# The end of a four-layer kernel: which engine does a 20-tap convolution and the gates' second product, and in which order

## The chip, the cores and the metric

The kernel runs on one core of a Trainium2 chip. A core has five engines, each with its own in-order queue of instructions: TensorE (PE in the profile; PEld is its weight load), VectorE (DVE), ScalarE (ACT), GpSimd (POOL) and SyncE (SP), which here issues transfers alone. TensorE writes to PSUM, which is split into eight banks of 128 partitions x 512 f32; the rest lies in SBUF. The metric is the device time of one execution in microseconds (us). Everything is f32.

## The reference, cut to what matters

The program is four layers of attention and feed-forward over 4096 tokens of 128 channels (8 blocks of 512 tokens). The change touches the last layer (layer 3) alone, which reads, for each block of tokens `x`:

```python
xn = layernorm(x)                     # attention: a causal depthwise convolution
h  = sum(table[:, i] * shift(xn, i) for i in range(1, 21))   # tap 0 is zero
x  = x + xn @ W1 + h @ W2 + bias
q  = fp4(layernorm(x))                # feed-forward, all operands rounded to fp4
g  = silu(q @ fp4(w_gate).T) * (q @ fp4(w_up).T)      # 352 wide
x  = x + fp4(g) @ fp4(w_down).T
```

`fp4` takes blocks of 16 numbers, scales each by its largest magnitude over 6, rounds to the eight fp4 magnitudes and scales back.

## The kernel before, in words

Layers 0 and 1 come first. Then `late()` (L1351) runs layer 2's attention as 64 frames (8 blocks x 8 pairs of heads), and hangs the other work on them: `at(frame, hook, f)` (L1369) puts a step into a frame, and the loop at L1984 calls the steps of its frame at four fixed places. Layer 3 of block b follows its attention by some frames; `planned` (L1822) gives every step of a block its frame. All instructions are issued in the order in which the code calls them (`manual_schedule`); each engine takes its own in that order, and an instruction that waits holds back all behind it on its engine.

When the 64 frames are over, `end()` (L1891) runs what is left in an order that is written out by hand. Left are: the last context and output product of attention; the feed-forward of block 6, called `L` below, from its gates on; and all of layer 3 for block 7, the last, in two halves: `A` (token tiles 0 and 1) and `B` (tiles 2 and 3). A tile is 128 tokens. The steps, each a function of `layer3` (L1647) or `norm_steps` (L1377):

- `stats` / `stats2` (L1382): VectorE's batch statistics, then on GpSimd the reciprocal root (L243, L244) and the shift (L1393). `scale` / `scale2` (L1395): ScalarE normalises, one activation per tile (L1399); the first one also adds the bias to `x` on GpSimd (L1407). `turn_` (L1414): TensorE transposes the tiles (L1417), ScalarE copies them into `xp`, the padded, channel-major input of the convolution (L1418).
- The convolution of a half, 20 taps. Taps 1 to 12 on TensorE: `conv_p` (L1685) multiplies shifted windows of `xp` with `tap_w[i]`, which is `W2` with each row scaled by tap i; these twelve matrices are made on ScalarE in frames 25 to 36 (`tap_weights` L1622, L1886 to L1889). Taps 13 to 16 on VectorE (`conv_v` L1662), taps 17 to 20 as ScalarE products (L1682) that GpSimd sums (L1683, `conv_s` L1673). `join` (L1698) adds the two sums, `conv_out` (L1709) multiplies the sum with `W2` into the same PSUM bank and adds the bank to `x` on VectorE (L1702). Blocks 0 to 6 have all taps on VectorE, ScalarE and GpSimd.
- `quant_x1` / `quant_x2` (L1722, L1726): fp4 of the normalised half. `fp4_scale` (L1255) is four VectorE instructions (L1265, L1267, L1268, L1270) and one of GpSimd (L1269); `fp4_round` (L1273) is four of VectorE (L1281, L1284, L1285, L1286) and a product on GpSimd (L1287). `turn_x` (L1730): transpose (L1733) and ScalarE copy (L1735).
- `gated(j)` (L1744): two 128x352 matmuls, then `tanh` on ScalarE into `s` (L1755; `s` has two buffers). `gated_v(j)` is `rest()` (L1757): two VectorE instructions, `(s+1)*gate` (L1758) and `s*0.5*up` into `h` (L1759).
- `quant_h1(i)`, `quant_h2(i)`: fp4 of a pair of `h` tiles, 704 wide; the scale and the scaled copy of this width have one buffer, so the next `quant_h1` waits until GpSimd has finished the product of the last `quant_h2`. `turn_h(i)` (L1784): three transposes per tile (L1790) and two ScalarE copies (L1793, L1796). `down` (L1798): twelve matmuls (24 in the profile, which counts an f32 matmul of this width twice) for a block, six for a half, the add to `x` on VectorE and the store.

PSUM in `late()` (L2016): two double banks `two` (the scores', `bank2()`), one bank `c`, one `o`, and two single banks `one` (`bank()`), used in turn. In `end()`, A's convolution takes `c` and B's takes `o`; the gates of A and B take double banks, and those of L take the single ones, which `turn_`, `turn_x`, `turn_h` and `down` use as well.

Of the kernel before, what the change touches and what calls it, by code (L numbers as in the profile page):

```python
# [24 lines left out]
P = 128  # L25
# [135 lines left out]
def body(ctx, tc, dram, spans, x_in, ib, it, ic, ei, out):  # L161
# [84 lines left out]
    def mm(out_, lhs, rhs, start=True, stop=True):  # L246
        nc.tensor.matmul(out_, lhs, rhs, start=start, stop=stop)  # L247
# [17 lines left out]
    def cols(t, j):  # L265
        return t[:, j * P : (j + 1) * P]
# [1084 lines left out]
    def late():  # L1351
# [11 lines left out]
        with tc.tile_pool(name="a2", bufs=2) as wp, tc.tile_pool(name="l3", bufs=1) as lp:  # L1363
# [255 lines left out]
            turned_taps = tuple(range(1, 13))  # L1619
            tap_w = {}  # L1620

            def tap_weights():  # L1622
                w = lp.tile([P, 4, TB], F32, tag="cg", name="tapw")
                for k, i in enumerate(turned_taps):
                    tap_w[i] = w[:, k // 4, (k % 4) * P : (k % 4 + 1) * P]
                    yield lambda i=i: nc.scalar.activation(
                        tap_w[i], l3["w2"], AF.Copy, scale=l3["taps"][:, i : i + 1]
                    )
# [18 lines left out]
            def layer3(b, xp, tile_, part=(0, J), conv_bank="one", h_tag="h"):  # L1647
# [37 lines left out]
                def conv_p(*taps):  # L1685

                    t["conv"] = ps = bank(conv_bank)
                    for j in range(j0, j1):
                        for i in (0, *taps):
                            mm(  # L1690
                                cols(ps, j),
                                xp()[:, pad - i + j * P : pad - i + (j + 1) * P],
                                tap_w[i] if i else l3["w1"],
                                start=(j == j0 and i == 0),
                                stop=False,
                            )
# [47 lines left out]
                def gated(j):  # L1744

                    h = tile_("h", h_tile)
                    if whole:
                        pg, pu = bank(), bank()
                    else:
                        two = bank2()  # L1750
                        pg, pu = two[:, 0, :], two[:, 1, :]
# [3 lines left out]
                    nc.scalar.activation(s, pg[:, :I3], AF.Tanh, scale=0.5)  # L1755

                    def rest():  # L1757
                        nc.vector.scalar_tensor_tensor(s, s, 1.0, pg[:, :I3], ALU.add, ALU.mult)  # L1758
                        nc.vector.scalar_tensor_tensor(  # L1759
                            h[:, j, :], s, 0.5, pu[:, :I3], ALU.mult, ALU.mult  # L1760
                        )
# [129 lines left out]
            def end():  # L1891
# [14 lines left out]
                L.gated(0)  # L1906
                A.scale()
                L.gated_v(0)
                A.turn_()
                L.gated(1)  # L1910
                B.scale()
                L.gated_v(1)
                B.turn_()
                L.gated(2)
                A.conv_p(*turned_taps)
                A.conv_v(*range(13, 17))
                A.conv_s(*range(17, 21))
                L.gated_v(2)
                L.gated(3)
                B.conv_p(*turned_taps)  # L1920
                L.quant_h1(0)
                B.conv_v(*range(13, 17))
                B.conv_s(*range(17, 21))
                A.join()
                A.conv_out()
                A.stats2()
                L.gated_v(3)
                L.quant_h2(0)
                B.join()
                A.scale2()  # L1930
                B.conv_out()
                B.stats2()
                A.quant_x1()
                A.quant_x2()
                L.turn_h(0)
                B.scale2()
                L.quant_h1(1)
                A.turn_x()
                A.gated(0)
                A.gated(1)  # L1940
                B.quant_x1()
                B.quant_x2()
                A.gated_v(0)
                A.gated_v(1)
                B.turn_x()
                L.quant_h2(1)
                A.quant_h1(0)
                B.gated(2)
                B.gated(3)
                B.gated_v(2)  # L1950
                A.quant_h2(0)
                L.turn_h(1)
                B.gated_v(3)
                L.down()
# [91 lines left out]
```

## Time and profile before

| | us |
|---|---|
| median of three runs | 1515.44 (1513.49 to 1515.67) |
| the profiled execution, its own time | 1513.91 |
| its span, first to last instruction | 1512.1 |
| the frames end: last output product of attention done | 1445.5 |
| from there to the end of the span | 66.6 |

The times below are from the span's start. In the span TensorE is busy 94%, VectorE 68%, ScalarE 69% and GpSimd 42%. What happens in the last 67 us, by the order of time of the four engines:

| | starts at us |
|---|---|
| A's convolution on TensorE | 1453.18 |
| A's add of the convolution (VectorE L1702) | 1466.62 |
| B's add of the convolution | 1473.46 |
| B's input quantised from | 1480.00 |
| A's `h` quantised from | 1489.68 |
| B's `h` quantised from | 1497.57 |
| last add to `x` | 1508.70 |
| last store issued | 1509.15 |

A row of the order of time reads: start, duration, engine, line, operation, written tile <- read tiles, shape, count, and in brackets how long the engine had been idle and who released it.

### The profile page before, as it was taken

What the parts mean: (1) busy time and instruction counts of PE and PEld (TensorE: products, weight loads), DVE (VectorE), ACT (ScalarE), POOL (GpSimd) and SP (SyncE); (2) the same over time, 40 slices, a digit from 0 to 9 for tenths busy, and PEclk for the clock granted to TensorE, in tenths of its full rate; (3) what the DMA queues carried; (4) which work ended last, traced back from release to release, by engine and by line L of the source; (5) the groups of instructions that cost most, each with busy time, mean ns of one, the idle gap of its engine ahead of it and who ended that gap; (6) DMA issues with size and microseconds to landing.
All of it is one profiled execution on the core that took longest, in us unless ns stands there. A gap on an engine that the chain in (4) does not pass through costs nothing.

```text
span 1512.1 us, 22428 instructions
## 1 busy us (share of the span) xinstructions
PE 1416.4 (94%) x7782; PEld 681.7 (45%) x7782; DVE 1031.1 (68%) x2129; ACT 1047.6 (69%) x2141; POOL 642.4 (42%) x742
## 2 busy tenths in 40 slices
PE   7789999998789889999999999999999999999976
PEld 3652222222276655543444445444454454454454
DVE  6766667777476646661674397786886877868857
ACT  7869999988776545564876486776776767767632
POOL 6647666665564321110441163452442633514432
PEclk9999999999999889999999999999999999999996
DMA  5049999977311010000100000000000000000000
GB/s 182 1 63 129 133 126 129 130 117 106 106 64 29 11 29 1 0 1 0 28 1 1 1 1 7 1 1 8 1 1 8 1 8 1 0 8 1 1 8 14
DMA packets 25442, 55.11 MB, mean 36 GB/s; under 512 B 5265, under 2 KB 18129, under 8 KB 20850
## 3 DMA queue, kind: packets, MB, share of 16 engines
q1 hardware_dynamic: 24688, 51.99, 20.6%
q10 hardware_dynamic: 578, 1.57, 0.3%
q8 instruction: 62, 1.02, 0.3%
q14 instruction: 50, 0.41, 0.1%
q0 software_dynamic: 64, 0.13, 0.0%
HBM read 47.35 MB, written 6.32 MB: 35 GB/s over the span
## 4 chain that ended last, share of the span: by engine, by line
PE 68%; ACT 13%; DVE 11%; DMA 4%; issue 2%; POOL 1%; SPq 0%; DVEq 0%; POOLq 0%; ACTq 0%
PE ps L247 65%; ACT hm L556 5%; DMA gs<-gates 3%; ACT ex L1483 2%; ACT hm L555 2%; DVE pr L568 1%; DVE nm L1477 1%; DVE fm L1284 1%; ACT xn L1399 1%; POOL rs L244 1%; DVE s L702 1%; DMA gates<-eq 1%; DVE frc L1267 1%; ACT xn L713 0%; PE ps L1790 0%
## 5 line engine op out<-in xcount | busy, mean ns | idle before, releaser
L1483 ACT ACTIVATE ex<-ps,nm 128x512 f32<-128x512 f32 x512 | 346.3, 689 | 192.3 <-DVE nm L1477 192.3
L1477 DVE TENSOR_REDUCE nm<-ps 128x2 f32<-128x1024 f32 x256 | 300.6, 1215 | 48.2 <-PE ps L247 47.9
L247 PE MATMUL ps<-q,k 64*128 64x512 f32 x1024 | 258.5, 621 | 4.9 <-ACT ex L1483 4.0
L247 PE MATMUL ps<-ex,vs 128*64 128x512 f32 x1024 | 233.8, 598 | 0.0
L1498 POOL TENSOR_TENSOR vs<-v,sm 128x256 f32<-128x256 f32 x128 | 81.3, 635 | 338.0 <-DVE sm L1497 290.3
L574 POOL TENSOR_TENSOR acc<-acc,pr 128x512 f32<-128x512 f32 x119 | 166.4, 1399 | 108.0 <-DVE pr L568 103.2
L556 ACT ACTIVATE hm<-ps,blob_f 128x1536 f32<-128x1536 f32 x128 | 196.4, 1534 | 0.0
L247 PE MATMUL ps<-xt,blob_a 128*128 128x512 f32 x304 | 151.9, 626 | 0.1
L247 PE MATMUL ps<-h,w 32*128 32x512 f32 x1024 | 148.0, 639 | 3.7 <-DVE eq L467 2.0
L247 PE MATMUL ps<-hm,w 128*32 128x512 f32 x1024 | 136.4, 605 | 11.6 <-DVE pr L568 10.8
L247 PEld LDWEIGHTS ps<-q,k 64*128 64x128 f32 x1024 | 87.5, 186 | 131.2 <-issue 75.3
L568 DVE SCALAR_TENSOR_TENSOR pr<-ps,blob_f,gs 128x512 f32<-128x512 f32 x120 | 89.9, 749 | 74.8 <-PE ps L247 62.3
L1683 POOL TENSOR_TENSOR acs<-acs,prod 128x512 f32<-128x512 f32 (+1 forms) x104 | 129.9, 1249 | 14.3 <-ACT prod L1682 9.6
L247 PEld LDWEIGHTS ps<-ex,vs 128*64 128x64 f32 x1024 | 67.8, 136 | 144.5 <-issue 124.9
L555 ACT ACTIVATE hm<-ps,blob_f 128x512 f32<-128x512 f32 x128 | 88.1, 688 | 29.3 <-PE ps L247 29.1
L243 POOL TENSOR_SCALAR rs<-mv 128x4 f32<-128x4 f32 (+1 forms) x69 | 17.5, 254 | 208.8 <-DVE mv L1389 146.5
L1483 ACT ACTIVATION_READ_ACCUMULATOR ex<-ps,nm 128x1 f32 x512 | 105.6, 206 | 0.0
L1445 DVE TENSOR_TENSOR v<-ps,blob_bc 128x512 f32<-128x512 f32 x64 | 44.3, 692 | 70.7 <-PE ps L247 44.1
L247 PEld LDWEIGHTS ps<-xt,blob_a 128*128 128x128 f32 x304 | 53.0, 193 | 87.5 <-issue 60.2
L247 PEld LDWEIGHTS ps<-h,w 32*128 32x128 f32 x1024 | 40.9, 183 | 111.8 <-ACT hm L555 86.1
L247 PEld LDWEIGHTS ps<-blob_a,ct 128*128 128x128 f32 x512 | 67.0, 191 | 32.3 <-issue 29.2
L244 POOL TENSOR_TENSOR rs<-rs,half 128x4 f32<-128x4 f32 (+1 forms) x69 | 72.4, 1049 | 5.7
(292 smaller groups left out, 2267.6 us busy)
## 6 DMA issues: line engine op xcount, KB each, us to landing
gs<-gates SPq DMA_DIRECT2D x256, 128.0 KB
blob_f<-in_f SPq DMA_DIRECT2D x1, 2560.0 KB
blob_a<-in_a SPq DMA_DIRECT2D x1, 2056.0 KB
x<-in_x SPq DMA_DIRECT2D x8, 256.0 KB
gates<-eq SPq DMA_DIRECT2D x8, 256.0 KB
by_rows<-fxn SPq DMA_DIRECT2D x8, 256.0 KB
ge<-gates SPq DMA_DIRECT2D x4, 512.0 KB
out<-x SPq DMA_DIRECT2D x7, 256.0 KB
```

Source lines behind the costliest of these rows:

```text
L243: nc.gpsimd.tensor_scalar(t, var, EPS, None, ALU.add)
L244: nc.gpsimd.tensor_tensor(t, t, half[:, : t.shape[-1]], ALU.pow)
L247: nc.tensor.matmul(out_, lhs, rhs, start=start, stop=stop)
L555: nc.scalar.activation(hm[:, 0, :], p1, AF.Gelu, bias=bias)
L556: nc.scalar.activation(hm[:, 1:, :], p3, AF.Gelu, bias=bias)
L568: nc.vector.scalar_tensor_tensor(pr, po, f0["b2"][:, e : e + 1], gs, ALU.add, ALU.mult)
L574: nc.gpsimd.tensor_tensor(acc[:, b, :], acc[:, b, :], pr, ALU.add)
L1445: nc.vector.tensor_tensor(v, pv, bias, ALU.add)
L1477: nc.vector.tensor_reduce(nm, ps, AX.X, ALU.max, negate=True)
L1483: nc.scalar.activation(ex[kt][:, i, :], ps[:, i, :], AF.Exp, bias=nm[:, i : i + 1], accum_out=sm[:, kt, i : i + 1],)
L1498: nc.gpsimd.tensor_tensor(vs[:, tiles, :, :], vs_[n][:, tiles, :].rearrange("p j (i n) -> p j i n", i=2), sm[:, tiles, :].unsqueeze(3).to_ ...
L1683: nc.gpsimd.tensor_tensor(t["acs"], t["acs"], p, ALU.add)
```

## The change

Five edits, all in `late()`:

1. `turned_taps` goes from taps 1 to 12 to taps 1 to 20; the eight more matrices are made by ScalarE in frames 37 to 44, four of them in a new tile `tapx` of 128x512.
2. In `end()`, `conv_p`, `conv_v`, `conv_s`, `join` and `conv_out` give way to `conv_tile(j)`, which does `W1` and all 20 taps of one tile on TensorE, and `conv_added()`, the add to `x`. (`conv_p` without taps stays for the other blocks.)
3. `gated(j, True)`, used for L, A and B in `end()`: ScalarE copies half of `up` from PSUM into a `prod` buffer, and GpSimd multiplies it with `s` into `h`, in place of VectorE's second instruction.
4. L's gates in `end()` take the double banks.
5. The order of `end()` is new. Among other things, `L.quant_h1(0)`, `L.quant_h2(0)` and `L.quant_h1(1)` stand ahead of A's add; A's `turn_x` behind B's second convolution tile; `L.turn_h(1)` and `L.down()` ahead of `A.gated_v(0)`; `A.quant_h1(0)`, `A.quant_h2(0)` behind B's gates and ahead of `B.gated_v(2)`.

```diff
@@ -1616,13 +1616,15 @@
 
             pad = 20
 
-            turned_taps = tuple(range(1, 13))
+            turned_taps = tuple(range(1, 21))
             tap_w = {}
 
             def tap_weights():
                 w = lp.tile([P, 4, TB], F32, tag="cg", name="tapw")
+                more = lp.tile([P, TB], F32, tag="tapx", name="tapx")
                 for k, i in enumerate(turned_taps):
-                    tap_w[i] = w[:, k // 4, (k % 4) * P : (k % 4 + 1) * P]
+                    part = w[:, k // 4, :] if k < 16 else more
+                    tap_w[i] = cols(part, k % 4)
                     yield lambda i=i: nc.scalar.activation(
                         tap_w[i], l3["w2"], AF.Copy, scale=l3["taps"][:, i : i + 1]
                     )
@@ -1682,18 +1684,33 @@
                             nc.scalar.activation(p, src, AF.Copy, scale=w)
                             nc.gpsimd.tensor_tensor(t["acs"], t["acs"], p, ALU.add)
 
-                def conv_p(*taps):
+                def conv_p():
 
                     t["conv"] = ps = bank(conv_bank)
                     for j in range(j0, j1):
-                        for i in (0, *taps):
-                            mm(
-                                cols(ps, j),
-                                xp()[:, pad - i + j * P : pad - i + (j + 1) * P],
-                                tap_w[i] if i else l3["w1"],
-                                start=(j == j0 and i == 0),
-                                stop=False,
-                            )
+                        mm(
+                            cols(ps, j),
+                            xp()[:, pad + j * P : pad + (j + 1) * P],
+                            l3["w1"],
+                            start=(j == j0),
+                            stop=False,
+                        )
+
+                def conv_tile(j):
+
+                    if j == j0:
+                        t["conv"] = bank(conv_bank)
+                    for i in (0, *turned_taps):
+                        mm(
+                            cols(t["conv"], j),
+                            xp()[:, pad - i + j * P : pad - i + (j + 1) * P],
+                            tap_w[i] if i else l3["w1"],
+                            start=(j == j0 and i == 0),
+                            stop=(j == j1 - 1 and i == turned_taps[-1]),
+                        )
+
+                def conv_added():
+                    added(t["conv"])
 
                 def join():
                     nc.vector.tensor_tensor(t["acc"], t["acc"], t["acs"], ALU.add)
@@ -1741,10 +1758,10 @@
                     flat = wide.rearrange("p a t -> p (a t)")
                     return flat[:, : J * I3].rearrange("p (j i) -> p j i", j=J)
 
-                def gated(j):
+                def gated(j, at_end=False):
 
                     h = tile_("h", h_tile)
-                    if whole:
+                    if not at_end:
                         pg, pu = bank(), bank()
                     else:
                         two = bank2()
@@ -1753,12 +1770,18 @@
                     mm(pu[:, :I3], cols(t["xt"], j - j0), wt["up"])
                     s = lp.tile([P, I3], F32, tag="s", name="s", bufs=2)
                     nc.scalar.activation(s, pg[:, :I3], AF.Tanh, scale=0.5)
+                    if at_end:
+                        u = block("prod", 3)()[:, :I3]
+                        nc.scalar.activation(u, pu[:, :I3], AF.Copy, scale=0.5)
 
                     def rest():
                         nc.vector.scalar_tensor_tensor(s, s, 1.0, pg[:, :I3], ALU.add, ALU.mult)
-                        nc.vector.scalar_tensor_tensor(
-                            h[:, j, :], s, 0.5, pu[:, :I3], ALU.mult, ALU.mult
-                        )
+                        if at_end:
+                            nc.gpsimd.tensor_tensor(h[:, j, :], s, u, ALU.mult)
+                        else:
+                            nc.vector.scalar_tensor_tensor(
+                                h[:, j, :], s, 0.5, pu[:, :I3], ALU.mult, ALU.mult
+                            )
 
                     t["rest", j] = rest
 
@@ -1903,55 +1926,51 @@
                 for h in (A, B):
                     h.added(outs[NB - 1])
                     h.stats()
-                L.gated(0)
+                L.gated(0, True)
+                L.gated(1, True)
                 A.scale()
+                A.turn_()
                 L.gated_v(0)
-                A.turn_()
-                L.gated(1)
+                L.gated(2, True)
                 B.scale()
                 L.gated_v(1)
+                L.gated(3, True)
                 B.turn_()
-                L.gated(2)
-                A.conv_p(*turned_taps)
-                A.conv_v(*range(13, 17))
-                A.conv_s(*range(17, 21))
+                A.conv_tile(0)
+                A.conv_tile(1)
                 L.gated_v(2)
-                L.gated(3)
-                B.conv_p(*turned_taps)
+                L.gated_v(3)
                 L.quant_h1(0)
-                B.conv_v(*range(13, 17))
-                B.conv_s(*range(17, 21))
-                A.join()
-                A.conv_out()
+                L.quant_h2(0)
+                L.quant_h1(1)
+                A.conv_added()
                 A.stats2()
-                L.gated_v(3)
-                L.quant_h2(0)
-                B.join()
+                L.turn_h(0)
+                B.conv_tile(2)
                 A.scale2()
-                B.conv_out()
-                B.stats2()
+                L.quant_h2(1)
+                B.conv_tile(3)
                 A.quant_x1()
                 A.quant_x2()
-                L.turn_h(0)
+                B.conv_added()
+                B.stats2()
+                A.turn_x()
+                A.gated(0, True)
+                A.gated(1, True)
                 B.scale2()
-                L.quant_h1(1)
-                A.turn_x()
-                A.gated(0)
-                A.gated(1)
+                L.turn_h(1)
+                L.down()
+                A.gated_v(0)
+                A.gated_v(1)
                 B.quant_x1()
                 B.quant_x2()
-                A.gated_v(0)
-                A.gated_v(1)
                 B.turn_x()
-                L.quant_h2(1)
+                B.gated(2, True)
+                B.gated(3, True)
                 A.quant_h1(0)
-                B.gated(2)
-                B.gated(3)
+                A.quant_h2(0)
                 B.gated_v(2)
-                A.quant_h2(0)
-                L.turn_h(1)
                 B.gated_v(3)
-                L.down()
                 B.quant_h1(1)
                 A.turn_h(0)
                 B.quant_h2_tile(1, 0)
```

In the built program nothing else moves: ahead of `end()`, the four engines' instructions stand in the same order as before, but for eight activations of 128x128 on ScalarE (L1626), one in each of frames 37 to 44.

## The prediction

> **What bounds the kernel now.** I read the profile from the coarse to the fine: the page's forty slices, a table by stage, the chain of work that ended last, and then the order of time, engine by engine, of the last 70 us. The slices (37.8 us each):
>
> ```profile
> PE   7789999998789889999999999999999999999976
> DVE  6766667777476646661674397786886877868857
> PEclk9999999999999889999999999999999999999996
> ```
>
> TensorE is full through the frames and slacks only in the last two slices, where its granted clock falls too: the frames belong to TensorE, the end to something else. The stages of the end (columns: stretch, its length, then busy time and count of PE, PEld, DVE, ACT, POOL, then clock, DMA share, GB/s):
>
> ```profile
> 1440.00:1460.00 20.00, 16.51 (x97) 11.16 (x97) 12.54 (x32) 6.76 (x16) 6.28 (x13) 1.00 0.05 14
> 1460.00:1480.00 20.00, 10.39 (x71) 8.96 (x70) 11.49 (x32) 5.03 (x14) 7.62 (x13) 0.72 0.00 0
> 1480.00:1500.00 20.00, 15.37 (x60) 11.23 (x60) 17.45 (x34) 4.36 (x13) 4.37 (x6) 0.76 0.05 14
> ```
>
> VectorE is busy 57% from 1460 to 1480 and 87% from 1480 to 1500. So the end waits first and is then bound by VectorE. The chain says for what (start, duration, what):
>
> ```profile
> 1451.89 14.71 PE ps L247 x116
> 1466.60 0.02 issue
> 1466.62 0.43 DVE x L1702
> ...
> 1471.81 0.35 DVE acc L1699
> 1472.16 0.04 issue
> 1472.20 1.24 PE ps L247 x4
> 1473.44 0.02 issue
> 1473.46 0.43 DVE x L1702
> ...
> 1488.26 1.39 POOL h L1287
> 1489.65 0.02 issue
> 1489.68 0.90 DVE fsc L1265
> ...
> 1497.57 0.90 DVE fsc L1265
> ```
>
> First 14.7 us of TensorE (gates and both convolutions) up to A's add, then VectorE steps up to B's add at 1473.46, then VectorE's long row of quantisations, broken once by GpSimd. From 1497.57 on, the quantisation of B's `h` to the last add at 1508.70 takes 11.13 us; the change leaves these steps alone, so what counts is **when VectorE can start the quantisation of B's `h`**.
>
> **How I sum.** I walked the old order of `end()` and the new one through, instruction by instruction: each starts when its engine is free and its inputs and buffers are there, with durations from the rows of the end and the hand-overs that the rows show (0.04 us between engines, 0.09 into GpSimd). One more thing is in the walk, from these two rows:
>
> ```profile
> 1502.09 0.87 POOL L1287 TENSOR_TENSOR h<-fa,fsc 128x352 f32<-128x352 f32 x1 [2.89 <-DVE fa L1286]
> 1502.35 0.81 DVE L1284 TENSOR_SCALAR fm<-fm 128x352 f32<-128x352 f32 x1
> ```
>
> L1284 of this width takes 0.34 us alone; here it took 0.81 and ended 0.20 after GpSimd's product. L1270 (two SBUF inputs) likewise took 1.57 instead of 0.89 beside a GpSimd sum at 1408.12. L1758, which reads PSUM, keeps its 0.51 beside GpSimd. So VectorE's instructions on SBUF alone (L1267, L1270, L1281 to L1286) are made to wait for a GpSimd product. The walk of the old order puts the last quantisation at 1497.48 (trace 1497.57) and the last add at 1508.49 (1508.70): good to 0.2 us.
>
> **Tap matrices in the frames.** Eight activations of 0.39 us (row L1626), 3.1 us of ScalarE in frames 37 to 44. Frames 25 to 32 carry one each and frames 41 to 48 none; the 64-frame output copies (L1518) lie 101.85 us apart over eight frames in both. Cost 0; TensorE, busy all of that time, hides them. If the cover were gone it would be 3.1 us.
>
> **Up to the convolution.** ScalarE now does tanh and copy for two L tiles ahead of `A.scale`. On a double bank tanh waits for both matmuls (A's L1755 starts at 1482.40, when `up` ends, 1482.37). L's second `up` ends at 1447.9, tanh and copy (0.47 each, overlapping by 0.1) end at 1448.8: `A.scale` slips by 0.55. The third tanh needs the `s` that GpSimd's first product frees; GpSimd does statistics until 1449.4, A's bias 0.73, the product 0.93, ending 1451.3. So `B.scale`, queued behind that tanh, slips from 1450.56 to 1452.1. But the convolution starts at 1453.2 as before (1453.18): then TensorE was held by L's third gates. Cost 0.
>
> **The copy** is bounded by the 256-wide (0.37) and 512-wide (0.59) PSUM copies; I take 0.47, the tanh row of the same 352 columns. **GpSimd's product**: bounded by its sums of 256 columns (0.73; the narrowest such row is 0.62) and 512 columns (1.28); between them, 352 gives 0.73 + 96 x 0.55/256 = 0.93, near the 352-wide rows with a broadcast operand (0.78, 0.87). VectorE's row for the step is 0.52. The Trainium skill, "GPSIMD Engine Reference", 4.1 Engine selection, speaks against this edit: elementwise work on two inputs belongs on VectorE, GpSimd being about half as fast; by it the product would be an estimated 1.04 us, which would make the sum 0.4 us worse.
>
> **The convolution.** 24 tap matmuls begin 2.68 us apart from the next group (1453.40 to 1456.08), 0.112 each; the `W1` pair takes 0.22. A tile now has 40 + 2: 0.22 + 40 x 0.112 = 4.69 us, against 2.90. Two tiles to 1462.7, `turn_h(0)` 0.7, two tiles to 1472.9. Gone are the wait of 5.6 us for A's `join` and the `conv_out` matmuls. B's add comes at 1473.0, **0.46 earlier**. A's convolution is done 4 us earlier, but its add stands behind `L.quant_h1(1)`, which waits 1.5 us for GpSimd's product (one buffer): A's add at 1465.1, 1.55 earlier. `turn_x` of A then stands on TensorE behind B's tiles, and its input is held 1.0 by GpSimd's product of `L.quant_h2(1)`: 1473.9, against 1478.50.
>
> **The new wait.** In the new order VectorE's add of `L.down` stands ahead of `A.gated_v(0)` and all that follows. From 1473.9: transposes and copy to 1474.8, four gate matmuls to 1477.4, tanh and copy of A's second tile to 1478.3, `B.scale2` 0.88 to 1479.1, copy of `L.turn_h(1)` to 1479.5 (it frees the bank of `down`), `L.down` 2.84 to 1482.4. VectorE has been idle since 1474.4: **8.1 us**, where the old order was busy. B's input is quantised from 1483.9, against 1480.00: **3.9 later**.
>
> **From there.** Old: 1480.00 to 1497.57, 17.57 us. New: B's input 3.3 (GpSimd's products of A hold it 0.4), `A.quant_h1` and `h2` 5.4 to 1492.6. B's gates start at 1489.6 on a TensorE that was idle since 1482.4; after such gaps the clock is 0.50 (1.45 us for a gate matmul where the row at 1479.65 has 1.54, 0.76 at full clock), rising after some 3 us of work as at 1482. Second tanh 1494.75, first product (L1758) 1495.3, GpSimd 1496.3, B's `h` quantised from **1496.37**. Walk against walk 1497.48 - 1496.37 = **1.1 us earlier**; the last add 1507.4 against 1508.5. As a check by work: VectorE loses 8 products (4.2 us), 8 tap instructions (3.7) and 2 joins (0.8) = 8.7, and gains some 7 us of waits and 0.6 of being held. ScalarE gives 8 tap products for 8 copies; GpSimd gives 6 sums (4.4) for 8 products (7.4).
>
> Sum: 1513.91 - 1.1 = 1512.8 for the profiled execution. It lay 1.5 below the median of the runs; against the median, 1515.44 - 1.1 = **1514.3**. A measurement of this kernel can tell about 0.2%, 3.0 us, from no change.
>
> **The rivals.**
> - *Half clock, slower.* TensorE has a gap of 1.5 us ahead of `L.down`, after gates with waits. For: the clock had fallen by 1469 with TensorE idle only since 1466.6. Against: over 1446 to 1452, busy about half, it stayed at 1.00. Price: `L.down` at 5.32 (row 1491.22) instead of 2.84, straight into VectorE's wait, and slow gates later: 2.1 slower than before, 1517.5; if it falls already at A's gates, 4.2, 1519.6. It decides from a clock below 1 between 1475 and 1482. The skill's "TensorE: Matmul & The Clock Gate", Part 1, has the clock fall after a whole idle window of about 3.4 us; by that this gap would not do it and the sum would stand.
> - *Full clock to the end, faster.* Less waiting on TensorE keeps it at 1.00: gates 0.5 earlier, last transposes and `down` 1.5 faster: 3.05, 1512.4. Against it: the tail's small steps are the same, and rows after 1500 show 0.50.
> - *Dear product.* 1.28 on GpSimd: 0.9 slower, 1516.3. At the other end, 0.62: 2.1 faster, 1513.4. Dear or cheap copy: 0.4 either way.
> - *The matrices aren't hidden.* 3.1 more: 1517.4; the equal frames speak against it.
>
> **Chances.** Forecast 0.62, full clock 0.13, half clock 0.13, dear product 0.07, matrices 0.05. The three runs lie 2.2 us apart, so part of each case crosses the bounds: faster 0.08 + 0.10 = 0.18; slower 0.07 + 0.02 + 0.01 = 0.10; the rest, 0.72, within 0.2%. The range goes from the full clock's 1512.4 less 0.8 of spread to the half clock's 1517.5.
>
> **What would show it.** TensorE without a gap from 1453.2 to 1472.9; A's add near 1465, B's near 1473; VectorE idle about 8 us ahead of L's add near 1482.4; B's input quantised near 1484, its `h` near 1496.4; GpSimd's new product near 0.93; L1267 at 1469.6 stretched to 1.1. I am wrong if L's add comes by 1479 (the order costs less) or past 1485 (clock), or if the frames end later than 1445.5.

## The result, and the profile after

The changed kernel takes **1517.06 us** (median of 20 runs, 1510.52 to 1525.09). Twenty runs of the kernel before beside it have a median of 1516.90 (1511.14 to 1523.02). The ratio is 1.0004, with a 95% interval from 0.9989 to 1.0019: no difference that these runs can show. The predicted time was 1514.3.

The profiled execution after took 1516.92 us, its span is 1515.1. The slices of its page, each 37.9 us:

```profile
PE   7789999998789989999999999999999999999994
DVE  6776677767476636651664397786886877877855
PEclk9999999999999889999999999999999999999997
```

Two things can be seen. The last but one slice of TensorE is full now (9 for 7): the convolution. The last one is emptier (4 for 6), VectorE's last two are both at half. One digit more differs in TensorE's row, where the change does nothing: slice 14 (492 to 530 us) is 9 for 8, and the clock's digit there is 8. This place comes up again below. By stage (the columns are those of the prediction's table):

```profile
1440.00:1460.00 20.00, 17.62 (x106) 12.09 (x106) 6.45 (x20) 9.38 (x24) 7.29 (x14) 1.00 0.05 14
1460.00:1480.00 20.00, 18.15 (x155) 17.32 (x154) 16.39 (x37) 2.22 (x7) 8.38 (x13) 1.00 0.01 1
1480.00:1500.00 20.00, 11.30 (x53) 7.60 (x51) 10.81 (x21) 5.77 (x18) 5.78 (x9) 0.83 0.05 13
```

From 1460 to 1480 TensorE (18.15 of 20, before 10.39) and VectorE (16.39, before 11.49) are now both busy for most of the stretch and the clock is 1.00 (0.72). The gain of this stretch is given back in the next: VectorE falls from 17.45 to 10.81. The order of time on VectorE says where:

```profile
1477.50 0.41 DVE L1719 TENSOR_TENSOR x<-x,ps 128x256 f32<-128x256 f32 x1
1477.95 0.48 DVE L1387 BATCH_NORM_STATS2 s<-x 128x6 f32<-128x128 f32 x2
1478.35 0.30 DVE L1389 BATCH_NORM_AGGREGATE mv<-s 128x2 f32<-128x6 f32 x2
1478.68 0.17 DVE L1391 TENSOR_SCALAR nb<-mv 128x2 f32<-128x2 f32 x1
1487.00 0.69 DVE L1719 TENSOR_TENSOR x<-x,ps 128x512 f32<-128x512 f32 x1 [8.15 <-PE ps L247]
1487.61 0.94 DVE L1778 SCALAR_TENSOR_TENSOR s<-s,ps 128x352 f32<-128x352 f32 x2
1488.47 0.41 DVE L1265 TENSOR_REDUCE fsc<-xn 128x16 f32<-128x256 f32 x1
```

After B's add and statistics VectorE does nothing for 8.15 us. It waits for `L.down` on TensorE, while A's gates (L1778), whose second tanh ended at 1482.4, stand behind. The chain that ended last (start, duration, what; pieces under 0.2 us left out) shows the two prices of the end:

```profile
1479.31 2.65 PE ps L247 x8
1482.00 0.34 issue
1482.34 0.46 ACT prod L1775
1482.80 0.76 ACT xn L1399 x2
1483.55 0.26 ACT ht L1816
1484.02 2.96 PE ps L247 x24
1487.00 0.69 DVE x L1719
...
1496.36 0.90 DVE fa L1286
1497.39 1.38 POOL h L1287
1498.78 1.79 POOL h L1780 x2
1500.59 0.90 DVE fsc L1265
```

It goes through all that `L.down` waits for, and then, ahead of the quantisation of B's `h`, through three GpSimd products in a row, two of them the new L1780.

**Where to count from.** The frames end 4.15 us later in the profile after: the last output copy of the frames (ScalarE L1518) starts at 1447.87, before at 1443.72. The first of these 64 copies is late already, at 574.45 against 570.23; between the first and the last lie 873.49 us before and 873.41 after. So the offset arises ahead of 570 us, where both kernels have the same instructions. What the change does is read from the last copy on. I call the stretch from its start to the start of the last add the **end**: 64.98 us before, 63.85 after, **1.1 less**, as the walk had it.

### The profile page after: what moved, and what is told of

It is laid out like the page before. It is cut to its first block, busy times and chain, and to the rows that moved or that the text cites. A ratio compares the mean times of both kernels' runs of the same rounds, so it can differ in the third digit from the quotient of the medians.

```text
span 1515.1 us, 22529 instructions
## 1 busy us (share of the span) xinstructions
PE 1422.2 (94%) x7838; PEld 687.5 (45%) x7838; DVE 1024.0 (68%) x2111; ACT 1047.6 (69%) x2149; POOL 645.6 (43%) x744
## 4 chain that ended last, share of the span: by engine, by line
PE 67%; ACT 15%; DVE 11%; DMA 4%; POOL 2%; issue 2%; SPq 0%; POOLq 0%; DVEq 0%; ACTq 0%
PE ps L247 64%; ACT hm L556 6%; DMA gs<-gates 3%; ACT hm L555 3%; ACT ex L1483 2%; DVE nm L1477 1%; DVE pr L568 1%; POOL rs L244 1%; ACT xn L1399 1%; DMA gates<-eq 1%; DVE s L702 1%; DVE fa L1270 1%; DVE fsc L1265 1%; DVE fm L1284 1%; ACT xn L713 1%
## 5 line engine op out<-in xcount | busy, mean ns | idle before, releaser
L247 PE MATMUL ps<-hm,w 128*32 128x512 f32 x1024 | 136.4, 605 | 11.1 <-DVE pr L568 10.3
L1685 POOL TENSOR_TENSOR acs<-acs,prod 128x512 f32<-128x512 f32 x98 | 125.5, 1281 | 7.9 <-ACT prod L1684 3.5
```

The source lines that it names most:

```text
L1685: nc.gpsimd.tensor_tensor(t["acs"], t["acs"], p, ALU.add)
```

## The experiments

The theory: the steps of the end were sized rightly; the misplaced wait of VectorE gives back most of what the edits save; and the total can't show the rest because layer 1, not the end, scatters. Rivals: the end itself scatters; GpSimd's products or the clock, not the wait, eat the gain; VectorE's work bounds the end. All of them, with the times from the start of the last output copy (the tail is from the start of the quantisation of B's `h` to the last add):

| run | B's `h` from | tail | end | median of its runs, ratio to before |
|---|---|---|---|---|
| before, first and second profile | 53.85, 53.72 | 11.13, 10.22 | 64.98, 63.94 | |
| after, first and second profile | 52.72, 52.74 | 11.12, 11.13 | 63.85, 63.86 | 1517.06, 1.0004 |
| l_add_later | 48.54 | 11.08 | 59.62 | 1514.52, 0.9968 (0.9950 to 0.9986) |
| products_dve | 50.56 | 11.12 | 61.69 | 1513.86, 0.9964 (0.9941 to 0.9987) |
| later_and_dve | 44.46 | 11.13 | 55.58 | 1508.96, 0.9938 (0.9917 to 0.9959) |
| old_order_taps | 53.48 | 10.20 | 63.68 | one run |
| old_order_products, the same again | 61.00, 57.33 | 11.13, 11.12 | 72.13, 68.45 | 1521.18, 1.0048 (1.0020 to 1.0076) |
| new_order_12taps | 61.24 | 11.13 | 72.36 | one run |
| after_warm, after_warm_2 | 53.88, 52.75 | 9.77, 9.61 | 63.65, 62.36 | one run each |
| best_order | 43.04 | 11.12 | 54.16 | 1506.62, 0.9939 (0.9914 to 0.9963) |
| best_order_warm | 43.04 | 10.52 | 53.56 | 1510.36, 0.9944 (0.9921 to 0.9968) |
| steady_before, steady_after | 53.82, 52.75 | 11.13, 11.12 | 64.95, 63.88 | 1523.44, 1522.96 |
| steady_best | 43.05 | 11.12 | 54.17 | 1512.18 |
| no_bias_before, no_bias_after | 53.80, 52.77 | 9.61, 11.13 | 63.41, 63.91 | 1511.30, 1510.96 |

### The same kernels once more

> The kernel before, unchanged, profiled once more. What is compared in all these runs is the END: from the start of the last output copy (ScalarE, 128x512, the last one of the frames) to the start of the last residual add on VectorE. It was 64.98 us in the first profile of before and 63.84 in that of after. Theory (the end repeats, the level does not: layers 0 and 1 with their gathers shift everything behind them): the end is again 65.0 within 0.3, while the last output copy lies anywhere from 1440 to 1455. Rival (the end itself scatters by microseconds, so that the 1.1 us between the two profiles are chance): the end differs by more than 1 from 64.98.

> The changed kernel, unchanged, profiled once more. Theory: its end is again 63.8 within 0.3, VectorE idle 8.1 to 8.2 us ahead of the add of L, the add of L 34.9 to 35.1 behind the start of the last tap matmul's convolution start being no different; and the place where its level leaves that of before lies ahead of 570 us. Rival (the end scatters): an end of 65 or more, or of 62.5 or less.

B's `h` comes at 53.72 and 52.74: the two orders repeat within 0.13, and the 1.0 to 1.1 between them is no chance. The end after repeats too, 63.86. That of before doesn't, 63.94 for 64.98: its last transposes and `down` met a clock of 1.00 in part. The expectation for before (within 0.3) failed, and the rival's mark (more than 1 from 64.98) is just passed: 1.04, of which 0.91 lies in the tail. So the end of before does scatter by about a microsecond, in its tail; the start of B's `h` does not.

### L's add behind B's input

```diff
-                L.turn_h(1)
-                L.down()
                 A.gated_v(0)
                 A.gated_v(1)
                 B.quant_x1()
                 B.quant_x2()
+                L.turn_h(1)
+                L.down()
```

> The changed kernel with L.turn_h(1) and L.down() moved from ahead of A.gated_v(0) to behind B.quant_x2(). TensorE, ScalarE and GpSimd keep their order; only VectorE's add of L stands later. Theory (the add, waiting 8.15 us for TensorE and ScalarE, blocks work on VectorE that is ready, and this wait ate what the rest of the change had won): by the walk the first product of A starts 6.3 earlier, B's input is quantised 4.8 earlier, B's h 4.6 earlier; the end is 59.2 (4.6 less than 63.84), if TensorE's gates of B run at full clock half a us less. Rival (the end is bound elsewhere, by GpSimd's products and TensorE's clock; the wait is only where slack shows): the end stays within 1 us of 63.8. Whole program: 4.6 us faster than after, 5.7 than before, ratio 0.996.

The end is 59.62 (expected 59.2), 4.2 less than after; the whole program 0.9968 (expected 0.996). Only VectorE's order differs, so the wait at this place costs the changed kernel 4.2 us. The same instructions on VectorE in this run:

```profile
1474.40 0.17 DVE L1391 TENSOR_SCALAR nb<-mv 128x2 f32<-128x2 f32 x1
1477.36 0.52 DVE L1778 SCALAR_TENSOR_TENSOR s<-s,ps 128x352 f32<-128x352 f32 x1 [2.79 <-ACT prod L1775]
...
1482.72 0.69 DVE L1719 TENSOR_TENSOR x<-x,ps 128x512 f32<-128x512 f32 x1 [0.30 <-PE ps L247]
...
1492.13 0.89 DVE L1265 TENSOR_REDUCE fsc<-h 128x44 f32<-128x704 f32 x1 [2.48 <-POOL h L1780]
```

The wait of 8.15 is gone: L's add waits 0.30, and 2.79 of waiting for A's gates are left. What is late next is in the last row: B's `h` waits 2.48 us for GpSimd's products.

### The second product back on VectorE

```diff
-                    if at_end:
-                        u = block("prod", 3)()[:, :I3]
-                        nc.scalar.activation(u, pu[:, :I3], AF.Copy, scale=0.5)
...
-                        if at_end:
-                            nc.gpsimd.tensor_tensor(h[:, j, :], s, u, ALU.mult)
-                        else:
-                            nc.vector.scalar_tensor_tensor(
+                        nc.vector.scalar_tensor_tensor(
```

> The changed kernel with the second product of the gates back on VectorE (reading PSUM, as before); ScalarE's eight copies and GpSimd's eight products are gone, the double banks, the convolution and the new order stay. Theory (in this order the products on GpSimd are a loss: 0.93 instead of 0.52 us each, ScalarE's tanh waits for the buffer that GpSimd frees, and VectorE had time for them): by the walk A's add comes 2.2 us earlier, the add of L 2.2 earlier, the end is 1.3 shorter, 62.5. Rival (VectorE bounds the end, so that giving it eight products of 0.52 back costs up to 4.2): the end is 65 to 68.

> Both in one: L.turn_h(1) and L.down() behind B.quant_x2(), and the second product of the gates on VectorE. Theory (two separate prices, the misplaced wait 4.2 to 4.6 us and the products on GpSimd, which cost more once nothing waits: 4.3 by the walk): B's h quantised 44.6 behind the last output copy, against 52.7 in the changed kernel, and an end of 54.9, 8.9 less than 63.85; whole program about 0.993 of before. Rival (VectorE is the bound as soon as the wait is gone, and eight products of 0.52 are on it again): the end is 59.6, that of the add moved alone, or up to 4.2 more.

Taking the products back from GpSimd shortens the end by 2.2 in the changed order (the walk had 1.3), and by 4.0 where L's add stands later (59.62 to 55.58; the walk had 54.9). The rival, that VectorE is the bound, expected 65 to 68 and is out. A product takes 0.93 on GpSimd and 0.52 on VectorE, and it is a link of the chain, not work beside it. In `later_and_dve` the quantisation of B's `h` waits for nobody:

```profile
1496.10 0.52 DVE L1774 SCALAR_TENSOR_TENSOR s<-s,ps 128x352 f32<-128x352 f32 x1
1496.65 0.52 DVE L1775 SCALAR_TENSOR_TENSOR h<-s,ps 128x352 f32<-128x352 f32 x1
1497.27 0.89 DVE L1265 TENSOR_REDUCE fsc<-h 128x44 f32<-128x704 f32 x1
```

### One edit at a time

`old_order_taps` is the kernel before with `conv_tile` twice in place of each `conv_p`, `conv_added` for each `conv_out`, and no `conv_v`, `conv_s` and `join`. `old_order_products` is the kernel before with this, and with `True` in the eight calls of `gated` in `end()`:

```diff
-                def gated(j):
+                def gated(j, at_end=False):
+                    if at_end:
+                        u = block("prod", 3)()[:, :I3]
+                        nc.scalar.activation(u, pu[:, :I3], AF.Copy, scale=0.5)
...
+                        if at_end:
+                            nc.gpsimd.tensor_tensor(h[:, j, :], s, u, ALU.mult)
```

`new_order_12taps` is the changed kernel with the old convolution, its steps put where the new ones stand:

```diff
-                A.conv_tile(0)
-                A.conv_tile(1)
+                A.conv_p(*turned_taps)
+                A.conv_v(*range(13, 17))
+                A.conv_s(*range(17, 21))
...
-                A.conv_added()
+                B.conv_v(*range(13, 17))
+                B.conv_s(*range(17, 21))
+                A.join()
+                A.conv_out()
...
-                B.conv_tile(2)
+                B.conv_p(*turned_taps)
...
-                B.conv_tile(3)
...
-                B.conv_added()
+                B.join()
+                B.conv_out()
```

> The convolution alone, in the old order: all twenty taps of the last block by TensorE, tile by tile, no tap work on VectorE, ScalarE and GpSimd, no joins; gates, products and order as before. Theory (this edit takes 4.5 us of work off VectorE where VectorE waits for TensorE anyway, and the convolution of B ends when it did): A's add about 4 us earlier (18.9 behind the last output copy, against 22.91), but B's add at 29.7 as before, B's h at 53.8, an end of 64 to 65. Rival (the work taken off VectorE shortens the end): B's h at 50 or earlier.

> The products alone, in the old order with the old banks: the second product of the gates of L, A and B by ScalarE's copy and GpSimd; the convolution and the order as before. Theory (a product on GpSimd is a longer step of the same chain): B's h 0.8 later than before, 54.6 behind the last output copy against 53.8, the end 0.8 longer (65.0 to 65.8). Rival (VectorE is freed of 4.2 us of products in its long row from 1474 to 1497): B's h at 51 or earlier.

> The products alone in the old order, once more, and timed. In its first profile the granted clock stood at 0.50 from 1457 to 1466, where it was 1.00 in every other profile, and the end was 72.1 instead of 65.0 to 65.8. Theory (the product as such costs 0.8; the rest was the clock, which fell once at an unlucky place, and the delays behind it): with the clock at 1.00 up to the first join, B's h 54.6 behind the last output copy and an end of 65 to 66; the median of the runs within 3 us of before. Rival (this kernel always loses the clock there, since TensorE waits in its gates, or the products cost that much without it): an end of 70 or more again, the median 6 or more above before.

> The changed kernel with the convolution of before (twelve taps on TensorE, four on VectorE, four by ScalarE and GpSimd, joins), put at the same places of the new order. Theory (the new order places quant_h of L early and the adds late, and stands only because VectorE has no tap work between): A's add 6.4 later than in the changed kernel, B's add 7.4 later, B's h about 5.9 later (58.6 behind the last output copy), the end 69.7, more if TensorE's clock falls meanwhile (up to 78). Rival (the tap work fits into VectorE's wait of 8.15 us): the end stays within 1 of 63.85.

The convolution alone brings A's add 3.8 us forward (19.12 behind the last copy, before 22.91), B's add nothing (29.68 for 29.75), B's `h` 0.2 to 0.4: worth next to nothing in the old order, as expected. The new order without it is 8.5 us worse at the end (72.36), more than the 5.9 expected, though within the 78 allowed for a fallen clock. A's add comes at 29.30: VectorE's tap work for it stands behind `L.quant_h1(1)`, which first waits 2.75 us for GpSimd, busy with sums and products. Over 468 to 476, when TensorE waits, the clock is at 0.50. So the edits of the convolution and of the order need each other.

The products alone missed both expectations. The first profile met a clock of 0.50 from 1457 to 1466; the second didn't, and still B's `h` is 3.5 later than before, not 0.8, and the median 3.4 us higher. The rows of the second profile:

```profile
1489.54 0.52 DVE L1761 SCALAR_TENSOR_TENSOR s<-s,ps 128x352 f32<-128x352 f32 x1 [1.82 <-ACT prod L1758]
1489.98 0.52 DVE L1281 TENSOR_SCALAR fm<-fa 128x704 int32<-128x704 int32 x1
1490.53 1.14 DVE L1284 TENSOR_SCALAR fm<-fm 128x704 f32<-128x704 f32 x1
...
1498.41 1.13 DVE L1284 TENSOR_SCALAR fm<-fm 128x704 f32<-128x704 f32 x1
...
1503.85 0.89 DVE L1265 TENSOR_REDUCE fsc<-h 128x44 f32<-128x704 f32 x1 [1.42 <-POOL h L1763]
```

B's add is 1.1 later than before. From there: 1.82 and 0.32 of waiting for A's gates, whose second pair met half clock, twice 0.6 in which L1284 (0.53 alone) is held beside a GpSimd product, 1.42 of waiting for the last product, less the four products of 0.52 that VectorE no longer does and 0.27 that it waited for A's gates in before: 1.1 + 2.1 + 1.2 + 1.4 - 2.1 - 0.3 = 3.4, near the 3.5 measured. The walk had put the holding and the waits too low.

### The clock at the end

```diff
+                def warm(n):
+                    ps = bank("c")
+                    for k in range(n):
+                        mm(cols(ps, 0), l3["w1"], l3["w1"], start=True, stop=True)
...
                 L.down()
+                A.warm(20)
...
                 A.down()
+                A.warm(15)
```

> The changed kernel with idle matmuls (W1 by W1, 128x128, into the bank of A's finished convolution, read by nothing) on TensorE: 40 behind L.down and 30 behind A's down. Theory (TensorE's clock falls in its idle stretches of 5.7 and 4.4 us and costs some 2 us of the end): the clock stays at 1.00 through B's gates and the last transposes, B's gate matmuls 0.76 instead of 1.54 and 1.38, B's h 0.6 earlier, the tail from there 10.0 to 10.3 instead of 11.1, the end 61.8. Rival (the clock is not on the path, or the added matmuls stand in the way): an end of 63.8 or more.

> The changed kernel with idle matmuls on TensorE of half the number: 20 behind L.down (4.5 us in the 5.7 it waits) and 15 behind A's down (3.4 in 4.4). Theory: clock 1.00 through B's gates and the last transposes, B's h 52.1 to 52.3 behind the last output copy instead of 52.7, the tail 9.8 to 10.2 instead of 11.1, the end 62.0 to 62.4. Rival (the clock falls all the same, or is not on the path): 63.8.

`after_warm` had 40 and 30. I had counted one record of 0.112 us for each, and there are two; so they stood in the way and B's `h` came 1.2 later. With the right number:

```profile
1482.80 4.63 PE L247 MATMUL ps<-blob_l 128*128 128x128 f32 x40
1489.60 0.86 PE L247 MATMUL ps<-wt_gate,xt 128*128 128x352 f32 x2 [0.46 <-ACT xt L1752]
1490.30 0.76 PE L247 MATMUL ps<-wt_up,xt 128*128 128x352 f32 x2
...
1496.60 0.89 DVE L1265 TENSOR_REDUCE fsc<-h 128x44 f32<-128x704 f32 x1 [2.48 <-POOL h L1780]
1504.61 1.56 PE L247 MATMUL ps<-wd,ht 128*128 128x128 f32 x12
```

B's gates take 0.86 and 0.76 (after: 1.54 and 1.38), the last `down` 1.56 (2.77). The tail is 9.61 instead of 11.12, the end 1.5 shorter. B's `h` comes no earlier, against the 0.5 expected: it now waits 2.48 us for GpSimd's products (1.09 in after), which set its place, not the gates.

### A better order

> The second product on VectorE, all taps on TensorE, L's add just ahead of the quantisation of B's h, and the order otherwise taken from the walk: L's first quantisation done while TensorE still convolves A, A's add ahead of L's second quantisation, that one cut in two around A's input, L's transposes late. Theory (the walk, which has put every step within 0.5 us so far): A's add 17.4 behind the last output copy, B's add 26.9, B's input quantised at 31.6, its h at 42.2, an end of 52.5 to 53, some 3 less than the 55.58 of the add moved and the products back; about 0.992 of before. Rival (TensorE, done with all it can do, idles at half clock and gives it back): an end of 55 or more.

> The same with idle matmuls to hold the clock: 26 behind the gates of B and 12 behind A's down. Theory: the tail from the quantisation of B's h to the last add 10.0 to 10.3 instead of 11.1, the end 1 us shorter than that of the same order without them. Rival (the last transposes are held by GpSimd's products, and matmuls in front of them only delay them): the end the same or longer.

With the products on VectorE, the order from `L.gated(0)` on is, in short: `L.quant_h1(0)`, `L.quant_h2(0)` ahead of the convolution; `A.conv_added` with its statistics and `A.scale2` ahead of `L.quant_h1(1)`; `L.quant_h2(1)` behind the quantisation of A's input; `L.turn_h(1)`, `L.turn_h(0)`, `L.down` around B's input, and the add of `down`, split off, ahead of `B.quant_h1(1)`. The end is 54.16, 9.7 us shorter than after, though 1.2 more than hoped: each step comes 0.6 to 0.9 later than walked. The ratio, 0.9939, is that of `later_and_dve` within the intervals. Holding the clock as well takes 0.6 off the end (tail 10.52; 1 was expected), which the runs don't show (0.9944).

### Where the runs scatter

The fifteen profiles with layer 1 as it is, sorted by the granted clock from 484 to 526 us (layer 1), with the start of the first output copy of the frames:

| clock, 484 to 526 | first copy at |
|---|---|
| 0.92 | 568.72 |
| 0.88 (before) | 570.23 |
| 0.84 | 570.16, 570.35, 572.22, 573.08 |
| 0.80 (after, twice) | 574.45, 573.90 |
| 0.76 | 574.44 |
| 0.71 | 579.27 |
| 0.63 | 579.09, 578.11, 578.78 |
| 0.57, 0.55 | 580.40, 579.44 |

The stretch holds four one-row matmuls that lay biases into PSUM (`ones` times a row of 512; 3.70 us together in before, at a clock of 1.00). In each of the fifteen profiles the granted clock falls to 0.50 between 1.0 and 4.3 us after the first of them starts, and stays there for 3.4 us or a multiple of it: 3.4 in before, 10.2 in after, 30.7 in `best_order`. To take the clock out, `steady_*` put four matmuls of the identity behind each of the four of `chosen_biases`, and `no_bias_*` leave these four out:

```diff
 # steady
                         mm(c_["two"][m][:, k, :], ones, rows[name], stop=False)
+                        keep_clock(4)
 # no_bias
-                        mm(c_["two"][m][:, k, :], ones, rows[name], stop=False)
...
-                    mm(two[:, 0, :], cols(xm, m), l1["ew1"], start=False)
+                    mm(two[:, 0, :], cols(xm, m), l1["ew1"])
```

> The kernel before with four matmuls of the identity by itself, into a bank that nothing reads, behind each of the four one-row bias matmuls of layer 1 (16 matmuls, 3.6 us of TensorE). Theory (the one-row matmuls don't hold the clock, and how long it stays down afterwards is a matter of phase, which makes the spread): the granted clock from 484 to 526 is above 0.9, the runs lie within 6 us instead of 12 to 15, and the median is no higher than before's in spite of the 3.6 us. Rival (the spread comes from transfers, or the clock follows something else): the same spread, and a median about 3.6 higher.

> The changed kernel with the same 16 matmuls at the same place. Theory: the same narrow spread; against steady_before the median is 0.1 to 1.1 us lower (B's h 1.0 to 1.1 earlier; the last 10 to 11 us the same, or 0.9 longer where before has a warm TensorE there). Rival (the change is worth several us in either sense and was only covered by the spread): a difference of over 2.5.

> The best order of the earlier runs (products on VectorE, L's add late, quantisations reordered) with the same 16 matmuls. Theory: its end is 54.2, so the median lies 9 to 11 below that of steady_before and within 6 us over the runs. Rival (its gain was partly the phase): less than 6 below.

> The kernel before without the four one-row bias matmuls of the chosen tokens in layer 1 (1x128 by 1x512, eb1 and eb2): the biases of these two products are left out, the products start their banks themselves. At full clock the four take 4.0 us. Theory (they make the clock fall, and the spread): the granted clock from 484 to 526 is above 0.9 in the profile, the runs lie within 6 us, the frames start at 561 to 566 instead of 570 to 580, the median 6 to 12 below before. Rival (the four only take their own time): a median 4 lower, the same spread of 12 to 16, the clock again anything from 0.55 to 0.9.

> The same in the changed kernel. Theory: as narrow a spread, the median 0.1 to 1.1 below that of no_bias_before. Rival: a difference of over 2.5 in either sense, which would mean that the change does something to the program outside the end.

The identity matmuls failed to hold the clock. In `steady_before` (stretch, its length, TensorE busy, then clock, DMA share, GB/s):

```profile
484.00:488.00 4.00, 3.12 (x16) 0.91 0.25 72
488.00:492.00 4.00, 4.00 (x12) 0.50 0.22 66
492.00:496.00 4.00, 4.00 (x12) 0.50 0.00 0
496.00:500.00 4.00, 4.00 (x12) 0.50 0.00 0
```

TensorE is busy without a gap and granted half. The median is 4.9 above that of before beside it (1518.54), and the three `steady` kernels spread over 8.0 to 9.3 us (twelve runs each, standard deviation 2.1 to 3.3), not within 6, where before spreads over 15.8 (29 runs, 4.2). In `no_bias_before`, without the four:

```profile
484.00:488.00 4.00, 3.12 (x26) 1.00 0.23 68
488.00:492.00 4.00, 4.00 (x29) 1.00 0.24 70
492.00:496.00 4.00, 2.71 (x12) 1.00 0.22 66
496.00:500.00 4.00, 3.11 (x20) 1.00 0.11 33
```

Its ten runs lie between 1510.07 and 1512.56, **2.5 us** apart (standard deviation 0.8), where the eighteen of before beside them span 12.0 (3.8); the nine of `no_bias_after` span 3.9 (1.4). The median is 7.0 lower, of which the four matmuls' own time is 3.7 (the expectation had 4.0). The clock over 484 to 526 is 0.88 and 0.84, not above 0.9 (it still falls near 500, and in `no_bias_after` from 493.6 to 497.0 as well), and the frames start at 567.96 and 567.41, not by 566: these two numbers missed, the spread didn't. So the four one-row matmuls make most of the spread. It is not their shape alone: other pairs of 1x128 by 1x512 stay in this stretch of `no_bias_before` and run at 1.00 (from 489.39, 1.12 us). That the four do it by way of the clock is argued from the two windows and the table, not shown: an execution with the biases in place and the clock at 1.00 I didn't get.

With the spread gone, the two kernels differ by 1510.96 - 1511.30 = **-0.3 us** (drawing the runs anew, the ratio lies between 0.9987 and 1.0009); under `steady`, by -0.5. `steady_best` is 11.3 below `steady_before`, a little more than its 9 to 11.

## Why the prediction was wrong, and where it was right

The steps, measured in the first profile after, each less the 4.15 us by which its frames ended later:

| step | predicted | measured |
|---|---|---|
| tap matrices in the frames | 0 | 0 (64 frames in 873.49 and 873.41) |
| GpSimd's product, ScalarE's copy | 0.93, 0.47 | 0.93, 0.46 |
| convolution starts | 1453.2 | 1453.07 |
| one tile of 42 taps | 4.69 | 4.69 (1457.22 to 1461.91) |
| A's add, B's add | 1465.1, 1473.0 | 1465.41, 1473.35 |
| L1267 held by GpSimd | 1.1 | 0.97 |
| A's `turn_x` | 1473.9 | 1474.26 |
| VectorE idle ahead of L's add; the add | 8.1; 1482.4 | 8.15; 1482.85 |
| B's input quantised | 1483.9 | 1484.32 |
| B's `h` quantised | 1496.37 | 1496.44 |
| last add | 1507.4 | 1507.56 |

The mechanism was right: the steps lie within 0.5 us of the walk, and B's `h` comes 1.0 to 1.1 us earlier in each of the four pairs of profiles. So was the likeliest case, a change too small to tell (0.72). Two terms of the number were not right.

**The step that failed is the last one, from the sum to the number.** The prediction put the walk's difference on "the median of the runs", three runs 2.2 us apart, and took "0.8 of spread". Over twenty runs that median is 1516.90, not 1515.44: 1.5 of the 2.8 us by which 1514.3 missed. The other 1.3 are the forecast gain of 1.1, which shows as +0.2 in runs whose interval goes from -1.7 to +2.9 us. In five later sets of 14 to 29 runs the kernel before has medians from 1517.81 to 1519.33 and spans 10.0 to 15.8 us. So the level was 1.5 to 4 us too low and the spread several times too small. The prediction's own warning sign, frames that end later than 1445.5, did show (1449.67), with a cause that lies in layer 1. The page of before had a hint: two eights in the clock's row, from 492 to 568 us. They say nothing of the change's worth, and much on whether it can be seen in a total.

**"11.13 us unchanged" holds for after alone.** All ten profiles of the new order and its variants without matmuls added at the end have a tail of 11.1. Before has 11.13, 10.22, 11.13 and 9.61. The steps are the same; the clock that TensorE's last transposes and `down` meet is not. Where the tail is 11.13, `L.down` takes 5.3 us, A's transposes behind it run at full clock (0.55) and B's last ones at half (0.90); where it is shorter, `L.down` takes 2.94 and it is the other way round. Why an execution takes one course or the other was not tried and stays open. That the first two profiles differ by just the 1.1 of the walk is luck in part, since that of before has the long tail: in the second pair the ends differ by 0.1. So the end of before is 63.4 to 65.0, that of after 63.9, and the worth of the change lies between 1.1 us and a loss of half a us.

The rivals: *half clock* did not happen (1.00 through `L.down`). *Full clock* was priced at 3.05; with idle matmuls it is 1.5, all in the tail. *Dear product* did not happen by its duration. But the prediction weighed only how long a product takes, within the walk it had, and never walked the change without it: the products on GpSimd cost 2.2 us where they stand. "GPSIMD Engine Reference", 4.1 Engine selection, of the Trainium skill, which the prediction cited against this edit, was borne out: 0.93 for 0.52, a factor of 1.8 (the page has about 2).

## What to carry to other kernels

An instruction that waits for another engine belongs behind all that is ready on its own: one add, 0.69 us long, cost 4.2 us by its place, half of the 8.7 us of work that the edits had taken off VectorE. Work moved to a slower engine pays only off the chain; ask for each moved product who waits for it, and walk the change without it as well. Before forecasting a microsecond, look where one kernel's executions differ from each other, and measure from a landmark behind that place.

## What was not expected of the hardware

- *One-row matmuls and the clock.* In layer 1 the granted clock falls to 0.50 while the rows show TensorE busy without a gap, 1.0 to 4.3 us after the first of four one-row matmuls (1x128 by 1x512): 4.00 busy of 4.00 at 0.50 from 488 to 500 in `steady_before`, 1.00 over the same stretch in `no_bias_before`, without them. How long it then stays down differs from run to run, from 3.4 to 30.7 us; over 94 runs of the kernel before (four of the five later sets), its time and its mean clock go together (0.968: 1527.3 us; 0.983: 1512.0; correlation -0.87).
- "TensorE: Matmul & The Clock Gate", Part 1, of the Trainium skill has the clock set over free-running windows of about 3.4 us and calls the ramp's cost less than 1% of a typical span, advising against a fit to a specific count of slow matmuls. The stretches at 0.50, all multiples of 3.4 us, agree with such windows. The runs of one kernel scatter here by up to 15.8 us of 1518, some 1%, and that is over ten times what was to be measured.
